# The last feed-forward of a twelve-layer decoder, taken as steps in the slots of the attention ahead of it

## The chip, the cores and the metric

The kernel runs on one core of one Trainium2 chip. The core has five engines with queues of their own: PE (TensorE, matmuls and transposes, results in PSUM), DVE (VectorE), ACT (ScalarE), POOL (GpSimd) and SP (SyncE, here a queue for DMA issues). The metric is the device time of one execution in microseconds (us): the median of the runs shown. The kernel before has 2451.33 us, the median of 3 runs from 2450.39 to 2455.79.

## The reference, cut to what matters

A residual stream x of shape (8, 256, 256) in f32 passes twelve sublayers, x = x + f(norm(x)). The last three count here:

```
x = x + L3_attn(layernorm(x))             # 16 heads of 16, causal, low-rank scores
h = rmsnorm(layernorm(x)) @ W_in.T + b_in  # L3_xattn; plus a smoothed, regathered context ctx
x = x + h + depool(rmsnorm(ctx), lens)
h = relu(layernorm(x) @ w1 + b1)           # L3_ffn: 256 -> 1024 -> 256
x = x + h @ w2 + b2
```

The output is x. Everything is f32, with 8 batches of 256 rows, 2048 rows in all.

## The kernel before, in words

**Layout.** x lies in SBUF as eight tiles x[b] of 128 partitions by 2 by 256 (the two halves of a batch's rows). xn holds the normed rows and xnT their transpose, 128 by 2 by 2048. Both are shared by all layers.

**Order.** The program is written in Python and a scheduler orders each engine's queue when it is built: of the instructions whose inputs are ready by its own model it takes the one that stands first in the program. A DMA or a POOL operation can so be issued ahead of others that the program lists earlier. While `self.pinned` is "both", which holds in `attend`, the PE and DVE instructions keep the order of the program; ACT, POOL and SP stay free. Tiles come from pools with a number of buffers for each name; a new tile waits until the last reader of the buffer that it takes over is done. A layer has a pool of its own in SBUF, left and right in turn, and PSUM pools (`banks`): in this attention 6 banks of name mm, each 128 by 512 f32.

**The attention's slots.** `attend` runs over slots n; one slot is one head of one batch, 8 x 16 = 128 of them, total = 128. In slot n PE makes the scores of head n (line 342), their maxima go through DVE (line 356), and the transposed scores of head m = n - lag, lag = 10, are made again with the maximum inside (line 373) and go through ACT's exponential (line 385). What else has to happen is put into a dictionary `todo` by slot: `prepare` (projections, 15 to 9 slots ahead of a batch), `together` every fourth slot (transposes of queries, `blend` with the values on line 396, `divide`), and what `finish`, `following` and `behind` add after a batch's last `divide`. Slots go on until todo is empty.

**The layer beside it.** `l3_xattn` has no slots of its own: its per-batch steps `beside` (load ctx, squares on ACT, scaling, smoothing, counting, places; slots 0 to 8 of a batch) and `behind` (product, add, second norm) are taken in the attention's slots. Batch b divides last in slot 16b + 31; `finish` needs 6 slots more, the norm that follows 8, then come the product 2 slots later and the second norm's parts 4, 6, 7, 10 and 12 slots later. For the last batch that is slots 143, 159 and 161 to 169. `ctx` has two buffers, and so the load of batch b + 2 waits for `scaled` of batch b.

**The last feed-forward.** `l3_ffn` is a layer of its own after the attention. It loads w1 and w2 into the ring of three weight buffers, b1 and b2 on ACT's queue, and adds b2 to every x[b] on POOL (line 1921, 8 operations). Then, for four blocks of 512 rows (two batches each): eight matmul pairs of w1 and xnT into a bank each (line 1926) with a Relu on ACT into fh (line 1927, two buffers of 16 KB a partition), and for each batch of the block two chains of eight matmuls of fh and w2 into one bank (line 1933) and one add to x on DVE (`add_to_x`, line 268). `store` then sends the eight x[b] out, 256 KB each, as each becomes ready (line 1939).

Lines 166 (`mm`), 71 (the wrapper of the pinned engines) and 268 are helpers, so many operations share them in the profile.

Of the kernel before, what the change touches and what calls it, by code (L numbers as in the profile page):

```python
# [21 lines left out]
F32 = mybir.dt.float32  # L22
# [9 lines left out]
P = 128  # L32
# [45 lines left out]
class Decoder:  # L78
# [214 lines left out]
        for i, (dst, wide, g) in enumerate(parts):  # L293
            self.nc.scalar.copy(dst, ps[:, i, :])  # L294

    def attend(self, pool, nh, dh, prepare, finish, scale=1.0, causal=False, beside=None, behind=None):

# [161 lines left out]
        while todo or now[0] <= total + lag + 1:  # L461
            n = now[0]
            m = n - lag
            if halves:
                score(n, 0), weigh(m, 0), score(n - 1, 1), weigh(m - 1, 1)
                peak(n - 1), exponentials(m - 1)
            else:
                score(n, 0), weigh(m, 0), score(n, 1), weigh(m, 1)
                peak(n), exponentials(m)
            for fn in todo.pop(n, ()):  # L470
                fn()
            now[0] += 1
        self.pinned = False

# [1238 lines left out]
    def l3_attn(self, pool):  # L1713

        nc, dram = self.nc, self.dram
        w = self.weights(dram["l3a_w"])
        wq, wo = k_of(w[:, :512], 2), k_of(w[:, 512:1024], 2)
        wqv = k_of(w[:, 1024:2048], 2)  # L1720
        wk = k_of(self.weights(dram["l3a_wk"])[:, :1024], 2)
        lsr = self.plain("l3a_lsr", pool)
        bq, bkw = self.plain("l3a_bq", pool), self.plain("l3a_bkw", pool)
        bv, bo = self.row("l3a_bv", pool), self.row("l3a_bo", pool)
        bqv = pool.tile([P, 512], F32, tag="bqv", name="bqv", bufs=1)
        nc.gpsimd.tensor_copy(bqv[:, D:], bv)
        nc.vector.tensor_tensor(
            bkw, bkw, self.cst[:, C_ONE17 : C_ONE17 + 1].to_broadcast([P, 4]), ALU.add
        )

        a = pool.tile([P, 2, P], F32, tag="a", name="a", bufs=1)
        wide_bq = pool.tile([P, 2, P], F32, tag="wide_bq", name="wide_bq", bufs=1)
        pa, pb = self.bank(2, P), self.bank(2, P)
        pw = self.bank(2, 2, P)
        for f in range(2):
            fs = slice(f * P, (f + 1) * P)
            self.mm(pa[:, f, :], (lsr[:, fs], lsr[:, D + f * P : D + (f + 1) * P]))
        heads = self.cst[:, C_HEADS : C_HEADS + P].unsqueeze(1).to_broadcast([P, 2, P])
        nc.vector.tensor_tensor(a, pa, heads, ALU.mult)
        nc.vector.tensor_copy(wide_bq, bq.unsqueeze(2).to_broadcast([P, 2, P]))  # L1740
        for f in range(2):
            for i in range(2):
                self.mm(pw[:, i, f, :], (wq[:, f, i * P : (i + 1) * P], a[:, f, :]))
            self.mm(pb[:, f, :], (wide_bq[:, f, :], a[:, f, :]))
        nc.vector.tensor_copy(wqv[:, :, :D], pw.rearrange("p i f n -> p i (f n)"))
        nc.vector.tensor_copy(bqv[:, :D], pb.rearrange("p f n -> p (f n)"))
        qs = self.wides("q", 3, 16, [16])
        vs = self.wides("v", 3, 16, [16])
        two = lambda r: r.unsqueeze(1).to_broadcast([P, 2, D])
        split = lambda r: r.rearrange("p (h d) -> p h d", d=16).unsqueeze(1).to_broadcast([P, 2, 16, 16])  # L1750

        def prepare(b):
            xT = self.xnT[:, :, b * S : (b + 1) * S]
            q, v = qs[b % 3], vs[b % 3]
            live = {}

            def project(t):
                qv = self.bank(512)
                self.mm(qv, *[(xT[:, k, t * P : (t + 1) * P], wqv[:, k, :]) for k in range(2)])
                for dst, c in ((q, 0), (v, D)):  # L1760
                    self.dve(nc.vector.tensor_tensor(
                        dst[:, t, :, :16], qv[:, c : c + D].rearrange("p (h d) -> p h d", d=16),
                        bqv[:, c : c + D].rearrange("p (h d) -> p h d", d=16), ALU.add,
                    ))

            def keys(j):
                if j == 0:
                    live["kT"] = pool.tile([P, 4, S], F32, tag="kT", name="kT", bufs=3)
                kT = live["kT"]
                pk = self.bank(2, S)  # L1770
                for i in range(2):
                    g = 2 * j + i
                    self.mm(pk[:, i, :], *[(wk[:, k, g * P : (g + 1) * P], xT[:, k, :]) for k in range(2)])
                for i in range(2):
                    g = 2 * j + i
                    nc.scalar.activation(kT[:, g, :], pk[:, i, :], AF.Identity, bias=bkw[:, g : g + 1])
                if j == 0:
                    nc.gpsimd.tensor_tensor(self.x[b], self.x[b], two(bo), ALU.add)
                return q, kT, v

            return [
                (15, lambda: project(0)), (13, lambda: project(1)), (11, lambda: keys(0)), (9, lambda: keys(1))
            ]

        def finish(b, o, later):
            oT = pool.tile([P, 2, S], F32, tag="oT", name="oT")

            def out():
                po = self.bank(2, D)
                for t in range(2):  # L1790
                    self.mm(po[:, t, :], *[(oT[:, k, t * P : (t + 1) * P], wo[:, k, :]) for k in range(2)])
                self.add_to_x(b, None, po)

            later(2, lambda: self.features(oT, o))
            later(4, out)
            return 6

        beside, behind = self.l3_xattn(pool)
        self.attend(pool, 16, 16, prepare, finish, 1.0 / math.sqrt(32.0), True, beside, behind)

    def l3_xattn(self, pool):


        nc, dram = self.nc, self.dram
# [36 lines left out]
        def beside(b):  # L1841
# [2 lines left out]
            live = {}  # L1844

            def squares():
                live["ctx"] = ctx = new("ctx", 2, 512)
                live["ss"] = ss = self.small.tile([P, 2], F32, tag="css", name="css")
                nc.sync.dma_start(ctx, dram["ctx"][b].rearrange("(h p) d -> p h d", p=P))
                for t in range(2):  # L1850
                    scalar.activation(self.junk, ctx[:, t, :], AF.Square, accum_out=ss[:, t : t + 1])
                gpsimd.tensor_scalar(ss, ss, 1.0 / 512, 1e-5, op0=ALU.mult, op1=ALU.add)
                gpsimd.tensor_tensor(ss, ss, self.minus, ALU.pow)

            def scaled():
                live["u"] = u = new("u", 2, D)
                for t in range(2):
                    vector.scalar_tensor_tensor(
                        u[:, t, :], live["ctx"][:, t, :D], live["ss"][:, t : t + 1], ginit, op0=ALU.mult, op1=ALU.mult
                    )  # L1860
# [32 lines left out]
        def behind(b, later):  # L1893
# [12 lines left out]
            later(2, product)  # L1906
            for wait, fn in zip((4, 6, 7, 10, 12), self.following(b, norm=after)):
                later(wait, fn)
            if b == B - 1:
                later(12, lambda: setattr(self, "next", after))  # L1910

        return beside, behind

    def l3_ffn(self, pool):
        nc, dram = self.nc, self.dram
        w1 = k_of(self.weights(dram["l3f_w1"]), 2)
        w2 = k_of(self.weights(dram["l3f_w2"]), 8)
        b1 = self.plain("l3f_b1", pool)
        b2 = self.row("l3f_b2", pool)
        for b in range(B):  # L1920
            nc.gpsimd.tensor_tensor(self.x[b], self.x[b], b2.unsqueeze(1).to_broadcast([P, 2, D]), ALU.add)
        for blk in range(4):
            hT = pool.tile([P, 8, 512], F32, tag="fh", name="fh")
            for i in range(8):
                ps = self.bank(512)
                self.mm(ps, *[(w1[:, k, i * P : (i + 1) * P], self.xnT[:, k, bass.ts(blk, 512)]) for k in range(2)])
                nc.scalar.activation(hT[:, i, :], ps, AF.Relu, bias=b1[:, i : i + 1])
            for j in range(2):
                po = self.bank(2, D)
                for t in range(2):  # L1930
                    c = (2 * j + t) * P
                    self.mm(
                        po[:, t, :], *[(hT[:, i, c : c + P], w2[:, i, :]) for i in range(8)],
                    )
                self.add_to_x(2 * blk + j, None, po)

    def store(self):
        for b in range(B):
            self.nc.sync.dma_start(self.out[b].rearrange("(h p) d -> p h d", p=P), self.x[b])

    def run(self):
# [11 lines left out]
        with tc.tile_pool(name="between", bufs=1, reuse_waits="tile") as self.between:  # L1955
            with tc.tile_pool(name="l1f_hbm", bufs=1, space=bass.MemoryType.DRAM) as self.hbm:
                self.layers(self.l1_ffn, self.l2_attn)
        self.layers(self.l2_xattn, self.l2_ffn, self.l3_attn, self.l3_ffn)
        self.store()

    def layers(self, *layers):
# [171 lines left out]
```

## Time and profile before

| | |
|---|---|
| median of 3 runs | 2451.33 us (2450.39 to 2455.79) |
| the profiled execution's own time | 2458.11 us |
| its span, first to last instruction | 2456.3 us |
| PE busy | 2255.6 us (92%), 11739 instructions |
| DVE / ACT / POOL busy | 1221.8 / 889.2 / 498.8 us |
| mean granted PE clock | 0.938 |
| last feed-forward's first matmul | 2339.69 us |
| its last matmuls' add on DVE | 2452.18 us |

Times inside the profile count from the span's start. A line of the timeline or of the chain has start, duration, engine, source line, operation, output <- input, the number of operations merged into it, and in brackets how long the engine was idle before it and what ended that. A line of the windows has, for each engine, busy time and number of instructions, then the granted PE clock as a share of the full one, the share of time in which the DMA engines were busy, and GB/s. "issue" is time in which nothing that the profile shows was waited for.

### The profile page before, as it was taken

The numbers are of one execution on the slowest core, as the hardware profiler recorded it, in microseconds if no ns is written. First come the engines' busy times: TensorE is split into PE (matmuls) and PEld (weight loads), VectorE is DVE, ScalarE is ACT, GpSimd is POOL, SyncE is SP. The second block draws the span as 40 slices with busy tenths as digits, with TensorE's granted clock in tenths as the row PEclk, the third lists the DMA queues.
The fourth block names the chain that finished last, engine by engine and source line by source line (L and its number), as shares of the span: only waits on it lengthen the run. The fifth ranks groups of instructions, "written<-read, shape, count | busy, mean of one in ns | idle before, by whom it ended". The sixth has DMA issues, their size and how long they took to land. (4 is left out here: it accounts for less than half of the span.)

```text
span 2456.3 us, 32071 instructions
## 1 busy us (share of the span) xinstructions
PE 2255.6 (92%) x11739; PEld 1438.1 (59%) x11739; DVE 1221.8 (50%) x3136; ACT 889.2 (36%) x2182; POOL 498.8 (20%) x712
## 2 busy tenths in 40 slices
PE   7888889999999999889899987866999989999999
PEld 4555555666655555555557864544665555566556
DVE  5666553434323235676566537984453234555400
ACT  3433422334211113466114426764552114434311
POOL 3211333221000002221125534440212100000010
PEclk9999999999999999899899996886999998899899
DMA  3000000001100000121515571100111010000000
GB/s 128 1 1 1 30 14 26 18 10 37 55 13 26 13 18 13 49 66 36 211 38 154 164 175 52 46 18 1 53 36 32 0 52 18 10 18 18 4 13 22
DMA packets 56539, 103.69 MB, mean 42 GB/s; under 512 B 7624, under 2 KB 40224, under 8 KB 54720
## 3 DMA queue, kind: packets, MB, share of 16 engines
q1 hardware_dynamic: 44688, 75.90, 9.1%
q0 software_dynamic: 7680, 20.98, 3.7%
q10 hardware_dynamic: 4016, 4.76, 0.6%
q8 instruction: 95, 1.56, 0.3%
q14 instruction: 60, 0.49, 0.1%
HBM read 84.64 MB, written 16.78 MB: 41 GB/s over the span
## 5 line engine op out<-in xcount | busy, mean ns | idle before, releaser
L166 PE MATMUL mm<-xnT,w 128*128 128x512 f32 (+1 forms) x1104 | 475.0, 576 | 1.4 <-ACT xnT L249 0.7
L342 PE MATMUL mm<-kT,qT 17*128 17x256 f32 (+2 forms) x1536 | 322.3, 413 | 15.7 <-DVE q L360 12.7
L166 PEld LDWEIGHTS mm<-xnT,w 128*128 128x128 f32 x1104 | 210.5, 193 | 200.9 <-issue 191.6
L373 PE MATMUL mm<-qT,kT 18*128 18x256 f32 (+2 forms) x1536 | 310.8, 407 | 1.4 <-ACT p L385 1.2
L385 ACT ACTIVATE p<-mm 128x512 f32<-128x512 f32 (+1 forms) x384 | 211.9, 561 | 264.0 <-PE mm L373 138.5
L360 DVE TENSOR_REDUCE q<-mm 128x2 f32<-128x512 f32 x256 | 172.3, 688 | 166.9 <-PE mm L373 148.8
L342 PEld LDWEIGHTS mm<-kT,qT 17*128 17x128 f32 (+1 forms) x1536 | 179.0, 193 | 115.0 <-issue 41.1
L557 ACT ACTIVATE hT<-mm 128x512 f32<-128x512 f32 x104 | 62.1, 597 | 431.0 <-PE mm L166 412.0
L558 DVE TENSOR_TENSOR hT<-hT,mm 128x512 f32<-128x512 f32 x104 | 71.4, 686 | 278.3 <-PE mm L166 278.2
L533 PE MATMUL acc<-w,hT 128*128 128x256 f32 x832 | 195.5, 379 | 1.0 <-DVE x L268 1.0
L533 PEld LDWEIGHTS acc<-w,hT 128*128 128x128 f32 x832 | 157.9, 190 | 62.9 <-issue 41.8
L373 PEld LDWEIGHTS mm<-qT,kT 18*128 18x128 f32 (+1 forms) x1536 | 172.8, 191 | 13.7 <-issue 5.2
L232 POOL TENSOR_SCALAR rstd<-mv 128x2 f32<-128x2 f32 x64 | 12.2, 191 | 816.9 <-DVE mv L228 466.8
L396 PE MATMUL acc<-p,v 128*32 128x256 f32 (+2 forms) x1536 | 141.1, 389 | 0.0
L268 DVE TENSOR_TENSOR x<-x,mm 128x512 f32<-128x512 f32 x40 | 27.3, 686 | 193.1 <-PE mm L166 193.0
L294 ACT COPY qT<-tp 128x256 f32<-128x256 f32 x256 | 83.7, 376 | 84.0 <-PE tp L290 83.0
L1295 POOL DMA_INDIRECT xg<-xd,token x96 | 93.1, 969 | 98.3 <-PE tp L1418 62.7
L356 DVE TENSOR_REDUCE q<-mm 128x1 f32<-128x128 f32 (+1 forms) x256 | 78.7, 352 | 56.4 <-PE mm L331 56.2
L166 PE MATMUL mm<-wall,xT 128*128 x384 | 101.1, 387 | 2.3 <-DVE xT L1420 1.2
L290 PE MATMUL tp<-ident,q 128*128 128x128 f32 x512 | 90.6, 299 | 3.3 <-ACT qT L294 1.9
L396 PEld LDWEIGHTS acc<-p,v 128*32 128x32 f32 (+1 forms) x1536 | 61.7, 122 | 47.0 <-issue 21.6
L290 PEld LDWEIGHTS tp<-ident,q 128*128 128x128 f32 x512 | 60.7, 149 | 44.6 <-issue 32.0
(428 smaller groups left out, 3842.4 us busy)
## 6 DMA issues: line engine op xcount, KB each, us to landing
wall<-in_l1f_w SPq DMA_DIRECT2D x8, 1536.0 KB
yd<-y SPq DMA_DIRECT2D x96, 128.0 KB
kT<-in_ctxK SPq DMA_DIRECT2D x16, 512.0 KB
v<-in_ctxV SPq DMA_DIRECT2D x16, 512.0 KB
w<-in_l0f_w SPq DMA_DIRECT2D x8, 768.0 KB
cT<-in_ctxT SPq DMA_DIRECT2D x8, 512.0 KB
ctx<-in_ctx SPq DMA_DIRECT2D x8, 512.0 KB
w<-in_l2f_w SPq DMA_DIRECT2D x3, 768.0 KB
```

The costliest lines, as they stand in the source:

```text
L166: self.pe(self.nc.tensor.matmul(out, lhsT=lhsT, rhs=rhs, start=i == 0, stop=i == len(pairs) - 1))
L290: self.pe(self.nc.tensor.transpose(ps[:, i, t * P : (t + 1) * P], flat[:, t, g * P : (g + 1) * P], self.ident))
L294: self.nc.scalar.copy(dst, ps[:, i, :])
L342: self.pe(nc.tensor.matmul(ps[n][:, S * t : S * t + w], lhsT=qTs[n // hp][r, t * P : (t + 1) * P], rhs=kT[r, g, :w], start=t == 0 or not c ...
L356: self.dve(nc.vector.tensor_reduce(to[:, t : t + 1], bank[:, cols], axis=AX.X, op=ALU.max, negate=True))
L360: self.dve(nc.vector.tensor_reduce(to, bank.rearrange("p (t s) -> p t s", t=2), axis=AX.X, op=ALU.max, negate=True))
L373: self.pe(nc.tensor.matmul(ps[m, 1][:, 256 * k : 256 * k + w], lhsT=kT[r, g, k * P : (k + 1) * P], rhs=qTs[m // hp][r, S - w :], start=k = ...
L385: nc.scalar.activation(p, bank[:, :n3], AF.Exp, scale=scale)
L396: self.pe(nc.tensor.matmul(acc[r, S - w :], lhsT=v[:, k, (G * hp + i) % nh, :], rhs=live_p[G * hp + i][:, 256 * k : 256 * k + w], start=k ...
L533: self.pe(nc.tensor.matmul(acc[:, t, :], lhsT=hT[:, t * P : (t + 1) * P], rhs=units[i][2], start=i == 0 and t % 2 == 0, stop=i == len(unit ...
L558: nc.vector.tensor_tensor(hT, hT, u, ALU.mult)
L1295: (engine or self.nc.gpsimd).indirect_dma_start(out=dst, out_offset=None, in_=src, in_offset=bass.IndirectOffsetOnAxis(ap=rows, axis=0))
```

## The change

`l3_ffn` becomes a function that the attention calls. It returns a generator of 48 steps and a function `biased(b)`. A step is one first product with its Relu (eight to a block) or one chain of eight matmuls of the second product (four to a block). `attend` gets the generator as `then` and takes one step at the end of each slot with m > total; the steps left over are taken in a row after the last slot. `biased(b)`, the POOL add of b2, is put 11 slots behind each batch's `last`, between its second norm's scaling (10) and its transposes (12). fh has one buffer and lies in the attention's pool, as b1 and b2 do; ctx and u get one buffer. The feed-forward's banks are the attention's six. The batch that ends last adds and stores its two halves singly.

```diff
@@ attend
+            if then and m > total:
+                next(then, None)
             now[0] += 1
@@ l3_attn
-        beside, behind = self.l3_xattn(pool)
-        self.attend(pool, 16, 16, prepare, finish, 1.0 / math.sqrt(32.0), True, beside, behind)
+        rest, biased = self.l3_ffn(pool)
+        beside, behind = self.l3_xattn(pool, biased)
+        self.attend(pool, 16, 16, prepare, finish, 1.0 / math.sqrt(32.0), True, beside, behind, rest)
+        for _ in rest:
+            pass
@@ l3_xattn
-                live["ctx"] = ctx = new("ctx", 2, 512)
+                live["ctx"] = ctx = new("ctx", 2, 512, bufs=1)
-                live["u"] = u = new("u", 2, D)
+                live["u"] = u = new("u", 2, D, bufs=1)
...
-            if b == B - 1:
-                later(12, lambda: setattr(self, "next", after))
+            later(11, lambda: biased(b))
@@ l3_ffn
-        w1 = k_of(self.weights(dram["l3f_w1"]), 2)
-        w2 = k_of(self.weights(dram["l3f_w2"]), 8)
         b1 = self.plain("l3f_b1", pool)
         b2 = self.row("l3f_b2", pool)
-        for b in range(B):
+
+        def biased(b):
             nc.gpsimd.tensor_tensor(self.x[b], self.x[b], b2.unsqueeze(1).to_broadcast([P, 2, D]), ALU.add)
...
+        def steps():
+            w1 = k_of(self.weights(dram["l3f_w1"]), 2)
+            w2 = k_of(self.weights(dram["l3f_w2"]), 8)
+            for blk in range(4):
+                hT = pool.tile([P, 8, 512], F32, tag="fh", name="fh", bufs=1)
+                for i in range(8):
+                    ps = self.bank(512)
+                    self.mm(ps, *[(w1[:, k, i * P : (i + 1) * P], self.xnT[:, k, bass.ts(blk, 512)]) for k in range(2)])
+                    nc.scalar.activation(hT[:, i, :], ps, AF.Relu, bias=b1[:, i : i + 1])
+                    yield
+                for j in range(2):
+                    po = self.bank(2, D)
+                    for t in range(2):
+                        c = (2 * j + t) * P
+                        self.mm(po[:, t, :], *[(hT[:, i, c : c + P], w2[:, i, :]) for i in range(8)])
+                        if blk == 3 and j == 1:
+                            self.add_to_x(7, t, po[:, t, :])
+                        yield
+                    if blk < 3 or j < 1:
+                        self.add_to_x(2 * blk + j, None, po)
+
+        return steps(), biased
@@ store
-        for b in range(B):
+        for b in range(B - 1):
             self.nc.sync.dma_start(self.out[b].rearrange("(h p) d -> p h d", p=P), self.x[b])
+        for h in range(2):
+            self.nc.sync.dma_start(self.out[B - 1, h * P : (h + 1) * P], self.x[B - 1][:, h, :])
@@ run
-        self.layers(self.l2_xattn, self.l2_ffn, self.l3_attn, self.l3_ffn)
+        self.layers(self.l2_xattn, self.l2_ffn, self.l3_attn)
```

## The prediction

> **What bounds the kernel now.** I read the page's busy shares first (PE 92%, all else at most 50%), then the chain of waits over the last 150 us, then the busy time by windows. The end of the chain:
>
> ```profile
> 2312.14 1.70 PE acc L396 x15
> 2313.84 1.05 PE tp L71 x4
> ...
> 2335.39 2.62 DVE xn L71 x2
> 2338.06 0.92 PE tp L71 x3
> 2339.05 0.59 ACT xnT L249
> 2339.69 112.39 PE mm L166 x384
> 2452.18 0.69 DVE x L268
> ```
>
> The last feed-forward is one unbroken PE run of 112.4 us that starts only when the last batch's second norm has been turned (the xnT copy at 2339.05). It is bounded by PE alone, so it gets no shorter; it can only start earlier. What lies ahead of it:
>
> ```profile
> 2306.00:2312.00 6.00, 6.00 (x35) 3.14 (x27) 1.45 (x5) 2.24 (x6) 0.88 (x2) 0.51 0.00 0
> 2312.00:2318.00 6.00, 6.00 (x34) 4.86 (x34) 1.64 (x6) 1.26 (x3) 0.00 (x0) 0.64 0.00 0
> 2318.00:2324.00 6.00, 3.75 (x19) 2.75 (x17) 3.26 (x9) 0.59 (x1) 0.88 (x2) 1.00 0.00 0
> 2324.00:2330.00 6.00, 4.13 (x14) 3.30 (x15) 1.70 (x6) 1.17 (x2) 0.88 (x2) 0.72 0.03 6
> 2330.00:2336.00 6.00, 2.37 (x11) 1.73 (x10) 2.40 (x6) 0.00 (x0) 1.53 (x3) 1.00 0.06 19
> 2336.00:2340.00 4.00, 1.66 (x5) 0.99 (x6) 2.00 (x2) 0.58 (x1) 4.00 (x4) 0.60 0.00 0
> 2340.00:2344.00 4.00, 4.00 (x6) 1.67 (x6) 0.00 (x0) 0.49 (x1) 4.00 (x5) 0.55 0.00 0
> 2344.00:2350.00 6.00, 6.00 (x16) 2.65 (x15) 0.00 (x0) 2.26 (x4) 1.23 (x2) 1.00 0.00 0
> ```
>
> The columns are window, length, busy time of PE, weight loads, DVE, ACT and POOL with counts, PE clock, and transfers. From 2318 to 2340 PE is busy 11.9 of 22 us, part of that at a low clock; then the feed-forward's first 4 us run at 0.55. That idle stretch is the drain of the attention: batch 7's chain of product, norm, product, norm with nothing beside it.
>
> **Where the steps land.** A step is taken when m > total, so n - 10 > 128: slots 139 to 169 (batch 7 divides in slot 143; its second norm is turned in slot 143+6+8+12 = 169). That is 31 of 48 steps. Slot 139's first work is the last blend, which ends at 2313.84, so the first step starts there.
>
> **PE from 2313.84 on.** In the view by tile each f32 matmul is two records. Block to block the feed-forward's own DVE adds stand at 2362.63 and 2390.18, 27.55 us apart, so four blocks are 110.2 us: a first-product step 1.72 us (its Relus are 1.72 apart), a second-product step 3.44 us. The attention's remaining PE work, by its full-clock pieces in the chain, is 4 turns x 0.44, features 0.44, one pair of transposes 0.22, two products x 3.65, out 1.92: 11.6 us. The clock is low until about 2316.3 (the spacing of the 128x256 records falls from 0.31 to 0.215 us there); that costs 2.5 us x 0.5 = 1.2 us. The sum is 123.0 us, and PE ends at 2436.8 instead of 2452.2: **-15.4 us**.
>
> TensorE: Matmul & The Clock Gate of the Trainium skill (section on the warmup) says the full clock returns after some 3.4 us of sustained work. Counted from 2313.84 that would be 2317.2 and 0.5 us more than the row gives; no row of before shows the gate with this mix.
>
> This needs PE never to wait in those slots. The tightest pair is features (slot 145) to out (147): two steps, 3.4 us, against the 0.59 us copy and 0.68 us PE wait seen at 2320. Out to turn (147 to 157) took 4.2 us and now has ten steps, 24 us. Blocks 0 to 2 read only batches 0 to 5, normed by slot 137; block 3 comes after slot 169, behind 5 steps (15.5 us) of block 2. ACT needs 0.69 us per step of 1.72, and no table load stands between its copy at 2339.05 and the first Relu. One buffer of fh costs nothing: a block's first Relu comes behind that block's first matmuls, which PE issues after the old block's last. DVE's eight adds run in PE's order.
>
> **The transfers.** The weights are taken from the ring in slot 139 of the program, but the queue's view shows them issued as soon as a buffer is free:
>
> ```profile
> 1983.79 0.33 SPq L125 DMA_DIRECT2D w<-in_l3f_w  x1
> 2015.56 188.24 SPq L1849 DMA_DIRECT2D ctx<-in_ctx  x6
> 2247.72 0.34 SPq L125 DMA_DIRECT2D w<-in_l3f_w  x1
> ```
>
> w1 passed six ctx loads that stood before it in the program; w2 follows the last key projection (its matmuls end at 2247.7), 64 us before slot 139. I cost both at nothing. The two bias loads (0.33 and 0.86 us of ACT's queue) move from 2327.8 to the head of the attention near 1848, where PE waits on DVE alone: nothing. If ACT were the bound there, 1.2 us.
>
> **One ctx buffer.** Load b+1 now follows `scaled` of b; before, load b+2 did, at the same moment. So seven loads instead of six stand behind a scale, each with ACT caught on its landing:
>
> ```profile
> 2169.32 0.63 ACT L1851 ACTIVATE junk<-ctx 128x512 f32<-128x512 f32 x1 [1.58 <-DMA ctx<-in_ctx]
> ...
> 2170.48 0.38 PE L166 MATMUL mm<-ends,ones 128*128 128x256 f16 x2 [0.38 <-ACT p L385]
> ```
>
> ACT's 1.58 us becomes 0.38 us of PE. One more: **+0.4** (0 to 3.7, the link of the DMA in the chain). u with one buffer is read two slots after it is written, 14 before the next: nothing.
>
> **The biases.** Eight POOL adds (1.26 us each) leave the end and follow each batch's second norm; six fall into full attention. POOL and DVE disturb each other:
>
> ```profile
> 2335.32 9.91 POOL L1921 TENSOR_TENSOR x<-x,row_l3f_b 128x512 f32<-128x512 f32 x8
> 2335.39 2.61 DVE L71 TENSOR_SCALAR xn<-x,mv,rstd 128x256 f32<-128x256 f32 x2 [1.09 <-POOL rstd L233]
> ```
>
> Alone the same two take 0.73. At 1891.87 four took 2.55 instead of 1.46 beside one such add, so one add costs DVE at most 1.1 us: 0 to 6.5 us in all. What is queued behind on DVE are the score maxima, which read PSUM; PE waited on DVE 0.5 us in all from 2020 to 2300, so DVE has room: **+0.2**. On POOL the next batch's root can wait 1.3 us, three slots (some 7 us) ahead of its reader. The 1.9 us that the adds cost the last norm go, inside the -15.4.
>
> **The tail.** Batch 7's halves are added and stored singly. Each half's output is half of one PSUM tile, so the second half's matmuls wait for DVE to read the first. The nearest row of PE behind a DVE read of 128x256 PSUM is
>
> ```profile
> 1993.41 0.42 DVE L1739 TENSOR_TENSOR a<-mm,cst 128x256 f32<-128x256 f32 x1 [2.89 <-PE mm L166]
> 1993.89 1.22 PE L166 MATMUL mm<-a,w 128*128 128x128 f32 x4 [0.52 <-DVE a L1739]
> ```
>
> that is +0.52 (0 if it is not ordered). The last add shrinks from 0.69 to 0.42 (-0.27) and the last transfer from 256 to 128 KB; 256 KB keep the engines busy for 0.7 us in the view of transfers, so -0.35. Net **-0.1** (-0.6 to +0.5).
>
> PSUM — Partial Sum Buffer of the Trainium skill (PSUM bank collisions raise a hardware error) says that two engines may not touch one bank in the same partitions at once, even at other columns; by it the 0.52 must be paid, and without it the end would be 0.5 us earlier. No row of before reads half a bank while the other half is written.
>
> **Memory.** The attention's pool gains 16 KB for fh and about 1 KB of rows and loses 6 KB (ctx, u). If a tile used early in it now shares bytes with the preceding layer, its set-up (1847 to 1862) waits until 1984, where PE idles anyway: 0 to 5 us. Nothing in the profile says so; I take 0.
>
> **Sum.** -15.4 + 0.4 + 0.2 - 0.1 = -14.9 us. The profiled execution took 2458.11 (span 2456.3), 6.8 above the median, and the sum gives 2443.2 for it. The stretch removed is a fixed order of latencies, so I take the same difference from the median: 2451.33 - 14.9 = **2436.4 us**.
>
> **Rivals.**
>
> *One ctx buffer stalls PE (slower).* If a square stands ahead of exponentials that PE needs at once, PE loses the whole landing: 7 x 3.67 = 25.7 us, net +10.8, 2462. It decides from 14.9/7 = 2.1 us per load. For it: DMA ctx has 2.4% of the chain's last 306 us. Against: five landings in the attention cost PE under 0.4 each.
>
> *w2 comes late.* The ring could give w2 the buffer of the attention's first weights, read last by out in slot 147, where the first second-product step stands. PE would wait for the load (2247.72 to about 2252, 4.2 us) and restart at the low clock (some 1.7 us, by 2340 to 2344): gain 9.0, 2442.3. Against it: in before w2 took the key weights' buffer.
>
> *The biases hold DVE.* All 6.5 us reach PE: gain 8.6, 2442.7. Against it: DVE is busy 3.3 to 7.6 of each 10 us there.
>
> *Washed out.* Low-clock windows at other places (2030 to 2040 at 0.68, 2100 to 2110 at 0.50) shift with any new stall; three more of 3.4 us at half clock, with the tile overlap of 5 us, eat 10 us: 2446 to 2451.
>
> **How the numbers follow.** 0.2% (about what a measurement of this kernel tells from no change) is 4.9 us. Chances: forecast 0.70 (own range 2431 to 2441), w2 late 0.09, biases 0.06, washed out 0.05, slower 0.10. Faster 0.70 + 0.09 + 0.06 = 0.85, same 0.05, slower 0.10. The range takes in the two partial gains and, below, a clock better than in the profile: 2430 to 2445, leaving out 0.15 and a little.
>
> **What would show it.** In the profile after: the first xnT,w matmul of the feed-forward near 2314; PE busy throughout 2318 to 2340 at clock 1.0; PE's last matmul 15 us earlier; w2 issued near 2248; seven ctx loads from 2015 on; POOL's bias adds some 38 us apart; a gap of half a microsecond before the last 16 matmul records. Wrong would be a PE wait on w2 or fh inside the slots, ACT waits on ctx above 2 us, or the attention from 2000 to 2312 longer by more than 2 us.

## The result, and the profile after

| | before | after |
|---|---|---|
| median | 2454.19 us (2449.9 to 2466.92, 22 runs) | 2443.55 us (2435.04 to 2455.36, 22 runs) |
| ratio, 95% interval | | 0.9957 [0.9945, 0.9968] |
| profiled execution, its span | 2458.11, 2456.3 us | 2436.07, 2434.3 us |
| mean granted PE clock | 0.938 | 0.941 |

The kernel is 10.6 us faster (7.9 to 13.5 by the interval). In a second comparison it had 2446.39 against 2455.62 us, ratio 0.9954 [0.994, 0.9968]. The two profiled spans differ by 22 us, twice that. Single executions of one kernel lie some 20 us apart, and the first 1850 us, ahead of the change, alone came out 7.8 us shorter in this profile, so the spans as such say little. I cut both traces at events that stand in both kernels and compare the stretches between them.

The events, each taken at its start but for the blend, are: the first add hT<-hT,mm on DVE in the feed-forward of the layer group before (about 1855 us), the issue of the attention's first weights (w<-in_l3a_w on SP), the first ctx load that waits for a scaling, the issue of w2, the end of the last blend, and the last add to x on DVE. Below, **run-in** is the first stretch, **head** the second, **last stretch** the one from the last blend to the last add.

| stretch, us | before | after | difference |
|---|---|---|---|
| run-in: first hT add to the attention's weights | 123.43 | 120.38 | -3.05 |
| head: to the first ctx load behind a scaling | 36.94 | 43.19 | +6.25 |
| to the issue of w2 | 232.16 | 232.89 | +0.73 |
| to the end of the last blend | 66.12 | 64.65 | -1.47 |
| last stretch: to the last add | 138.34 | 122.33 | -16.01 |
| tail: to the end of the span | 4.12 | 3.42 | -0.70 |
| sum | 601.11 | 586.86 | -14.25 |

The last stretch is what the change is about. The chain of waits of the kernel after, end of the span (start, duration, engine, tile or operation, line, number merged):

```profile
2308.55 3.63 PE mm L166 x8
2312.19 0.44 PE tp L71 x4
...
2323.17 0.44 PE tp L192 x4
2323.60 22.41 PE mm L166 x88
2346.01 0.44 PE tp L71 x4
...
2385.19 41.36 PE mm L166 x152
...
2426.64 0.43 DVE x L268
...
2427.12 3.74 PE mm L166 x16
...
2430.88 0.42 DVE x L268
```

Where before had the DVE norms and the short turns of the drain, PE now goes from matmul to matmul from the end of the last blend (2308.55) to 2426.55; the norms of batch 7 have left the chain. The busy time by windows of the same kernel (columns as in the prediction's table) gives PE all of its time, at the full clock:

```profile
2318.00:2340.00 22.00, 22.00 (x90) 16.39 (x89) 4.94 (x13) 3.22 (x5) 3.04 (x5) 1.00 0.04 12
```

Before, the same table had 11.9 busy us of 22. The one gap left stands ahead of the last 16 records. From the timeline of the kernel after:

```profile
2426.64 0.42 DVE L268 TENSOR_TENSOR x<-x,mm 128x256 f32<-128x256 f32 x1 [2.84 <-PE mm L166]
...
2427.12 3.72 PE L166 MATMUL mm<-w,fh 128*128 128x256 f32 x16 [0.58 <-DVE x L268]
2430.88 0.42 DVE L268 TENSOR_TENSOR x<-x,mm 128x256 f32<-128x256 f32 x1 [3.81 <-PE mm L166]
```

The queue of SP shows the transfers as forecast, seven ctx loads behind a scaling (one merged row) and w2 long before its first use:

```profile
2011.01 226.31 SPq L1855 DMA_DIRECT2D ctx<-in_ctx  x7
2243.90 0.34 SPq L125 DMA_DIRECT2D w<-in_l3f_w  x1
```

What was not forecast is the head. From the timeline of the kernel after:

```profile
1967.91 0.33 ACTq L138 DMA_DIRECT2D in_l3a_lsr<-in_l3a_lsr  x1
...
1978.29 0.44 ACTq L138 DMA_DIRECT2D in_l3x_gcol<-in_l3x_gcol  x1
1979.81 9.96 POOL L1781 TENSOR_TENSOR x<-x,row_l3a_bo 128x512 f32<-128x512 f32 x8 [1.55 <-DMA row_l3a_bo<-in_l3a_bo]
1985.75 1.62 DVE L1817 TENSOR_SCALAR win<-win,in_l3x_gcol 128x256 f32<-128x256 f32 x2 [6.68 <-DMA in_l3x_gcol<-in_l3x_gcol]
1989.03 1.23 PE L166 MATMUL mm<-a,w 128*128 128x128 f32 x4 [5.54 <-DVE a L1742]
```

The loads of the attention's rows (lsr and the others), which stood at 1847 to 1859 before, beside the earlier layer, are issued only at 1967.91. DVE then stands 6.68 us for gcol, and PE waits 5.54 us for the product `a` that is queued behind it on DVE (0.52 us before).

### The profile page after: what moved, and what is told of

It reads as the page before. It is cut to its first block, busy times and chain, and to the rows that moved or that the text cites. A ratio compares the mean times of both kernels' runs of the same rounds, so it can differ in the third digit from the quotient of the medians.

```text
span 2434.3 us, 32056 instructions
## 1 busy us (share of the span) xinstructions
PE 2241.4 (92%) x11739; PEld 1432.1 (59%) x11739; DVE 1217.8 (50%) x3137; ACT 888.0 (36%) x2182; POOL 500.1 (21%) x712
## 5 line engine op out<-in xcount | busy, mean ns | idle before, releaser
L374 PEld LDWEIGHTS mm<-qT,kT 18*128 18x128 f32 (+1 forms) x1536 | 172.9, 191 | 13.5 <-issue 4.9
L268 DVE TENSOR_TENSOR x<-x,mm 128x512 f32<-128x512 f32 (+1 forms) x41 | 27.5, 672 | 175.9 <-PE mm L166 175.9
```

Of the source, the lines that this page charges most:

```text
L374: self.pe(nc.tensor.matmul(ps[m, 1][:, 256 * k : 256 * k + w], lhsT=kT[r, g, k * P : (k + 1) * P], rhs=qTs[m // hp][r, S - w :], start=k = ...
```

## The experiments

All compare traces by the stretches above; times are medians with the ratio to the kernel before, run beside them. Where only one execution is given, the reading rests on its trace. In the compiled kernels the attention's pool ends at byte 217696 of a partition before and at 228992 after, and the earlier layer's hT tiles lie at 225248 to 229344: fh now covers 3744 of their bytes.

**fit: the pool kept clear of hT.** Names that are not alive together share buffers, so the pool ends at byte 224896, 352 short of hT. Nothing else of the changed kernel is touched.

```diff
-        a = pool.tile([P, 2, P], F32, tag="a", name="a", bufs=1)
-        wide_bq = pool.tile([P, 2, P], F32, tag="wide_bq", name="wide_bq", bufs=1)
+        a = pool.tile([P, 2, P], F32, tag="dep", name="a", bufs=3)
+        wide_bq = pool.tile([P, 2, P], F32, tag="dep", name="wide_bq", bufs=3)
...
-        li, lf, end = one_of("li", [B, S], I32), one_of("lf", [B, S]), one_of("end", [B, S])
+        li, lf = pool.tile([B, S], I32, tag="plug", name="li"), pool.tile([B, S], F32, tag="plug", name="lf")
+        end = one_of("end", [B, S])
```

> Computes the same; two small set-up pairs (a and wide_bq, li and lf) share buffers with tiles used later, so the attention's pool is 4 KB smaller and ends 352 bytes short of the preceding feed-forward's hT. Theory (the pool overlaps hT by 3.7 KB, and so all of its set-up is issued only when that layer's last hT is taken): the set-up is issued as in the kernel before, behind the layer's head; from the load of the attention's first weights to the first ctx load behind a scale takes 37 us as before instead of 43, the rest as in the changed kernel; 6 us less than the changed kernel, ratio to before 0.993. Rival (the two bias loads that were put ahead in ACT's queue delay the set-up): they stand there still, so no change, 43 us and a ratio of 0.9957.

Measured: 2444.64 us (2437.27 to 2455.14), ratio 0.9944 [0.9923, 0.9965]. Head 37.05 us, as before the change, and in the timeline of fit the loads stand beside the earlier layer again, the bias b2 among them:

```profile
1841.35 0.32 ACTq L138 DMA_DIRECT2D in_l3a_lsr<-in_l3a_lsr  x1
...
1851.21 0.34 ACTq L132 DMA_DIRECT2D row_l3f_b<-in_l3f_b  x1
```

Shared bytes are what moved the set-up. fh alone lies on hT, but the whole set-up came late. The run-in is 123.42 us, also as before the change: the 3.05 us that the kernel after had gained there are gone with the cause of the 6.25. The next run says why. The 6 us and the ratio of 0.993 that were expected did not come; the interval holds the 0.9957 of the kernel after as well, so the times alone do not show that fit is faster than it.

**pad_before: the kernel before, with a tile of 8 KB more, 640 bytes of it on hT.** No load is moved in the program, no step and no other buffer; the tile is not used further.

```diff
         self.attend(pool, 16, 16, prepare, finish, 1.0 / math.sqrt(32.0), True, beside, behind)
+        pad = pool.tile([P, 8, 256], F32, tag="pad", name="pad", bufs=1)
+        nc.gpsimd.memset(pad[:, 0, :1], 0.0)
```

> The kernel before with one thing more: an 8 KB tile in the attention's pool, of which one column is cleared at the end, so that the pool reaches 640 bytes into hT. Theory (overlap alone delays the set-up): 6 us slower than before, ratio 1.0025, the stretch from the first weights' load to the first ctx load behind a scale 43 us instead of 37, the end untouched. Rival (bias loads in ACT's queue): they are where they were, so 1.000 and 37 us.

Measured: 2458.65 us against 2459.85, ratio 1.0001 [0.9984, 1.0019]. The head grew to 40.51 us, so shared bytes alone delay the set-up and cost 3.6 us there, not the 6 that were expected; and the run-in shrank to 120.38, so that the sum of the two is 160.89 us against 160.37 and the time did not move. The delayed set-up takes POOL's adds of the row bo out of the earlier layer. In that layer each of its three turns from one block to the next has four DVE scalings, and before, one of the adds fell on them. The timeline of before, at the first turn:

```profile
1891.87 2.55 DVE L238 TENSOR_SCALAR xn<-x,mv,rstd 128x256 f32<-128x256 f32 x4 [1.22 <-POOL rstd L233]
1892.69 1.26 POOL L1778 TENSOR_TENSOR x<-x,row_l3a_bo 128x512 f32<-128x512 f32 x1
1894.16 0.87 PE L248 MATMUL tp<-ident,xn 128*128 128x128 f32 x4 [0.89 <-DVE xn L238]
```

and of after, at the same turn, where all eight adds stand at 1979.81:

```profile
1884.13 1.54 DVE L238 TENSOR_SCALAR xn<-x,mv,rstd 128x256 f32<-128x256 f32 x4 [1.22 <-POOL rstd L233]
1884.92 1.36 PE L248 MATMUL tp<-ident,xn 128*128 128x128 f32 x8
```

The scalings take 1.54 us instead of 2.55, and PE's wait of 0.89 us is gone; three such turns are the 3.05 us. SBUF — State Buffer of the Trainium skill (SBUF: two separate sides) calls the port pair that VectorE and GpSimd share an exclusive lock: of a GpSimd operation and a VectorE operation of the kinds that use the pair, the one that starts first has it for its whole instruction and the other stands. The 1.01 us lost here, beside an add of 1.26, fit that; which of the two started first the rows don't show.

**loads_behind: the changed kernel with the two bias loads behind the cross-attention's set-up**, to see whether they account for the other 2.7 us of the head (43.19 against 40.51).

```diff
-        rest, biased = self.l3_ffn(pool)
-        beside, behind = self.l3_xattn(pool, biased)
+        beside, behind = self.l3_xattn(pool, lambda b: biased(b))
+        rest, biased = self.l3_ffn(pool)
```

> The changed kernel with the set-up of the cross-attention written before that of the feed-forward, so that the two bias loads stand behind the loads of gcol, brow, ginit and the lengths on ACT's queue; the bytes shared with the earlier layer stay. Head is the time from the issue of the attention's first weights to the first ctx load behind a scale: 36.94 us before, 43.19 after, 40.5 with shared bytes alone. Theory (the two loads ahead of gcol cost the other 2.7 us): head 40.0 to 41.0, and DVE's wait for gcol gone or below 4 us. Rival (the rest comes from more bytes being shared, whatever the order of the loads): head 42.5 or more.

Measured: one execution of 2433.96 us, head 44.25 us, so the theory's 40.0 to 41.0 fell. The gcol load went out at 1974.30 and DVE waits 0.71 us for it, yet the head is longer. The timeline of loads_behind, DVE's queue:

```profile
1980.44 2.54 DVE L1817 TENSOR_SCALAR win<-win,in_l3x_gcol 128x256 f32<-128x256 f32 x2 [0.71 <-DMA in_l3x_gcol<-in_l3x_gcol]
1986.43 0.29 DVE L1823 TENSOR_SCALAR row_l3x_ginit<-row_l3x_ginit 128x256 f32<-128x256 f32 x1 [3.45 <-DMA row_l3x_ginit<-in_l3x_ginit]
1986.64 1.35 DVE L1834 CAST lf<-li 8x256 f32<-8x256 int32 x1
1988.02 1.63 DVE L1835 TENSOR_TENSOR_SCAN end<-one,lf 8x256 f32<-8x256 f32 x1
1989.69 1.17 DVE L1836 TENSOR_SCALAR lf<-end 8x256 f32<-8x256 f32 x1
1990.79 0.41 DVE L1742 TENSOR_TENSOR a<-mm,cst 128x256 f32<-128x256 f32 x1
```

The wait has moved to the next load of the set-up (3.45 us for ginit), and three more set-up operations now precede `a` on DVE. So the order of the bias loads isn't the cause by itself: with the set-up late, whichever of its loads lands last holds DVE, and `a` with it. What exactly makes the head 43.2 with the bias loads and 40.5 in pad_before no run shows. The rows have one candidate, the load of w1 (1 MB). In loads_behind it goes out ahead of ginit's load:

```profile
1977.97 0.33 SPq L125 DMA_DIRECT2D w<-in_l3f_w  x1
1979.06 0.39 ACTq L132 DMA_DIRECT2D row_l3x_ginit<-in_l3x_ginit  x1
```

In pad_before it goes out behind it:

```profile
1985.29 0.39 ACTq L132 DMA_DIRECT2D row_l3x_ginit<-in_l3x_ginit  x1
1986.69 0.34 SPq L125 DMA_DIRECT2D w<-in_l3f_w  x1
1990.39 0.29 DVE L1819 TENSOR_SCALAR row_l3x_ginit<-row_l3x_ginit 128x256 f32<-128x256 f32 x1 [0.97 <-DMA row_l3x_ginit<-in_l3x_ginit]
```

From ginit's issue to DVE's use of it are 7.37 us with w1 ahead and 5.10 without. In the kernel after it is gcol's load that stands behind w1 (1977.30 and 1978.29), and 7.46 us pass until DVE goes on.

**no_steps: the changed kernel with no step in a slot**; all 48 follow in a row.

```diff
-            if then and m > total:
+            if then and m > 2 * total:
```

> The changed kernel with all 48 steps behind the last slot instead of 31 in the slots; everything else of the change stays. Theory (the gain is PE's idle drain filled by steps): PE is idle again for some 10 of the last 25 us of the attention, PE's last stretch is 12 to 15 us longer than in the changed kernel (a few matmuls can still slip ahead of the last transposes, and the last norm is freed of the bias adds), and with the 6 us lost at the attention's head it is no faster than before: ratio 1.000 to 1.003. Rival (the gain comes from the moved biases and the single stores, the steps add little): ratio 0.996 to 0.998.

Measured: 2455.88 us (2444.09 to 2465.1, 12 runs), ratio 0.9981 [0.9962, 0.9999], between the theory's and the rival's. The last stretch is 132.40 us: the steps in the slots are worth 10.1 of the 16.0 us, less than the 12 to 15 expected, and the drain is back (windows of no_steps: PE, weight loads, DVE, ACT, POOL, clock, transfers):

```profile
2332.00:2338.00 6.00, 2.13 (x9) 1.66 (x10) 2.83 (x9) 0.77 (x2) 2.16 (x3) 0.76 0.01 3
2338.00:2344.00 6.00, 6.00 (x18) 4.60 (x17) 0.61 (x1) 0.41 (x1) 0.00 (x0) 0.67 0.00 0
```

The other 5.9 us come without any step. Part of it is seen in the timeline of no_steps: since the feed-forward is no longer a layer that begins after the attention, its first matmuls are issued while DVE still does the last norm.

```profile
2343.18 2.74 PE L166 MATMUL mm<-xnT,w 128*128 128x512 f32 x6
2346.93 0.30 PE L71 MATMUL tp<-ident,xn 128*128 128x128 f32 x1 [1.00 <-DVE xn L71]
```

**bias_only: the kernel before with the b2 adds taken after each batch's norm**, as in the change, and nothing else of it.

```diff
+            later(11, lambda: self.nc.gpsimd.tensor_tensor(self.x[b], self.x[b], b2.unsqueeze(1).to_broadcast([P, 2, D]), ALU.add))
...
-        for b in range(B):
-            nc.gpsimd.tensor_tensor(self.x[b], self.x[b], b2.unsqueeze(1).to_broadcast([P, 2, D]), ALU.add)
```

> The kernel before with the eight bias adds alone moved behind each batch's second norm; the feed-forward stays a layer of its own behind the attention. The stretch from the last blend's end to the last DVE add is 138.3 us before and 132.4 in the run without steps in the slots. Theory (the adds cost the last norm 1.9 us, and the rest of those 5.9 us is matmuls that slip ahead of the last transposes once the layer shares the attention's banks): 136.4 us. Rival (all of the 5.9 us come from the moved adds): 132.4.

Measured: one execution of 2454.45 us; last stretch 136.22, 2.1 us less than before. In its last norm the scaling of the two halves is back to the short time (timeline of bias_only):

```profile
2334.21 0.74 DVE L71 TENSOR_SCALAR xn<-x,mv,rstd 128x256 f32<-128x256 f32 x2 [1.09 <-POOL rstd L233]
```

So of the 5.9 us some 2.1 are the biases and 2.7 the early matmuls. The remaining 1.1 us no run takes apart; the rows point at the clock. The feed-forward's first 24 matmul records take 12.49 us in the kernel before (from 2339.69, at 0.55 to 2344) and the 24 from 2348.25 on take 10.46 in no_steps, where the clock is 1.00; against these 2.0 us, the last product ahead of them takes 1.0 us longer in no_steps.

**fit_banks: fit, with a PSUM bank of its own for the last half.**

```diff
+                        if blk == 3 and j == 1 and t:
+                            po = self.bank(2, D)
                         self.mm(po[:, t, :], *[(hT[:, i, c : c + P], w2[:, i, :]) for i in range(8)])
```

> As fit, and the last batch's two halves have a PSUM bank each. Theory (the second half's matmuls wait for DVE to read the first half because both lie in one bank's tile): the gap of 0.58 us before the last 16 matmul records is gone, 0.6 us less than fit in the profile's tail (last product's first matmul to the span's end), not resolved in the times, ratio 0.993. Rival (PE waits there for something else, fh or w2): the gap stays.

Measured: 2442.06 us (2440.57 to 2448.02), ratio 0.9932 [0.991, 0.9954]. In its timeline DVE's idle time between the two last adds is 2.96 us instead of 3.81, and PE's 0.58 us gap is gone:

```profile
2437.03 0.42 DVE L268 TENSOR_TENSOR x<-x,mm 128x256 f32<-128x256 f32 x1 [2.96 <-PE mm L166]
```

The gap came from the two halves' shared tile, which is one bank; whether the tile or the bank is what orders them, this run doesn't tell, since it parts both. PSUM — Partial Sum Buffer of the Trainium skill (PSUM bank collisions raise a hardware error) asks that engines be kept apart by bank and not by address. Keeping to that order cost 0.58 us here.

**bias_end: fit_banks, with the eight b2 adds after the attention** instead of behind each norm.

```diff
+        for b in range(B):
+            biased(b)
         for _ in rest:
             pass
...
-            later(11, lambda: biased(b))
```

> As fit_banks, with all eight bias adds behind the last slot instead of spread over the attention. From the first ctx load behind a scale to the load of w2 takes 232.2 and 231.3 us in the two kernels that add the biases at the end, and 232.6 to 233.3 in the four that spread them. Theory (the adds disturb DVE inside the attention): 231.7, some 1 us less than fit_banks, with the rest as there. Rival (the extra ctx load or the clock makes that difference): 232.6 to 233.3 still.

Measured: 2445.08 us in one execution. From the first ctx load behind a scaling to w2 232.64 us, to the last blend 64.64, last stretch 121.46; fit_banks has 232.61, 64.63 and 121.47. The adds in the slots cost nothing that these two traces show.

**ctx2: fit_banks with a second ctx buffer**, its space won by sharing three more names.

```diff
-                live["ctx"] = ctx = new("ctx", 2, 512, bufs=1)
+                live["ctx"] = ctx = new("ctx", 2, 512)
```

> As fit_banks, with two ctx buffers again; three more set-up tiles share buffers so that the pool keeps its size. Theory (one buffer adds a seventh load behind a scale, at 0.4 us of PE): six loads behind a scale instead of seven, PE's waits on the exponentials one fewer and 0.4 us less, the same stretch to w2 within 0.5 us. Rival (one buffer makes every square late): ACT's waits on ctx fall by more than 3 us and the stretch by more than 1.

Measured: 2439.09 us in one execution. ACT waits 9.5 us for six landings instead of 10.8 for seven (in the kernels before and after: 9.1 for six, 10.6 for seven), but PE waits hardly less. PE's waits for the exponentials, kernel ctx2 from 2018 to 2310 (us in total, times, longest):

```profile
PE mm L166 <- ACT p L386: 1.6, 5, 0.4
PE mm L374 <- ACT p L386: 1.2, 7, 0.2
```

the kernel after, with seven, from 2011 to 2300:

```profile
PE mm L166 <- ACT p L386: 1.5, 5, 0.3
PE mm L374 <- ACT p L386: 1.2, 7, 0.2
```

and fit_banks, with seven, from 1990 to 2450:

```profile
PE mm L166 <- ACT p L386: 1.7, 6, 0.5
PE mm L374 <- ACT p L386: 1.2, 7, 0.2
```

One wait fewer than fit_banks, as the theory had it, but 0.1 us and not 0.4.

The stretch to w2 is 1.2 us shorter in ctx2, outside the theory's 0.5, and the one to the last blend 1.6 us. The number of buffers doesn't sort the kernels, though: with two, the stretch to w2 is 232.16 us in the kernel before, 232.74 in bias_only, 231.33 in pad_before and 231.38 in ctx2; with one, 232.61 in fit_banks and 230.63 in loads_behind. The clock goes with it here: over the 240 us behind that ctx load its mean is 0.943 in ctx2 and pad_before against 0.935 in fit_banks, and in the 30 us from 270 us on, 1.00 in both against 0.94. So I put the 1.2 us down to the clock and not to the buffer.

**early: fit_banks with steps ten slots sooner.**

```diff
-            if then and m > total:
+            if then and n >= total:
```

> As fit_banks, with steps from slot 128 on, where the scores end, instead of 139: 42 of 48 in the slots. Theory (PE has no idle time left there, at most a low clock while the slots hold 18-row matmuls alone): from w2's load to the last DVE add 184 to 186 us instead of 186.1, ratio 0.991 to 0.993. Rival (more steps beside the second scores hold up the exponentials and the banks): 188 us or more and a ratio above 0.994.

Measured: 2437.2 us (2434.54 to 2451.69), ratio 0.9921 [0.9896, 0.9946]. Issue of w2 to the last add 185.36 us against 186.10 in fit_banks.

**The three beside each other**: after, fit_banks and early, with the same executions of the kernel before for all.

> The changed kernel, the same work, run beside the two tuned versions so that the three share their runs of the kernel before. Theory (the head of the last attention pays 6.2 us for the shared bytes, the end pays 0.5 us for the shared bank, and what the parts gain is 16.0 us): 10 to 11 us below before, ratio near 0.9957. Rival (the 0.9957 was a chance of the clock's windows): a ratio above 0.998 or below 0.993.

> The pool kept clear of the earlier layer and the last block's halves in two banks. Theory: 6.7 us below the changed kernel of the same call, ratio near 0.9930. Rival (the head's 6.2 us come back elsewhere, since PE then enters the attention with a colder clock): within 2 us of the changed kernel.

> The same, with the steps allowed ten slots sooner. From the traces of the first runs, issue of w2 to the last DVE add takes 185.4 us with the early steps and 186.1 without: theory (PE is full either way, so earlier steps only swap places): within 1.5 us of the kernel without early steps in this call. Rival (early steps remove a low-clock window near the start of the feed-forward): 3 to 6 us below it, ratio near 0.991.

| | median | ratio | first hT add to the end of the span |
|---|---|---|---|
| after_again | 2446.39 us (2440.14 to 2452.3, 11 runs) | 0.9954 [0.994, 0.9968] | 593.21 us |
| fit_banks_again | 2443.21 us (2433.78 to 2448.15, 8 runs) | 0.9942 [0.9923, 0.9962] | 589.04 us |
| early_again | 2441.87 us (2433.5 to 2445.47, 6 runs) | 0.9945 [0.9924, 0.9965] | 582.20 us |

The expectation of 6.7 us for fit_banks fell: it is 3.2 us at the medians and 4.2 in the traces. I had counted from the issue of the attention's weights and so missed the run-in; with it, 6.25 - 3.05 + 0.58 = 3.8 us, which lies between the two. Early and fit_banks are 1.3 us apart at the medians, within the 1.5 of the theory. All three beat the kernel before; the intervals don't separate them from each other.

## Why the prediction came out as it did

It gave 2436.4 us, a gain of 14.9, and the median is 2443.55, a gain of 10.6. Of the 7.2 us between, 2.9 are the kernel before itself, which had 2454.19 in this comparison and not 2451.33; 4.3 are a gain that is smaller. By its own steps:

- **Where the steps land, and PE from the last blend on: -15.4.** Right in size. The last stretch gave -16.0 with the 0.58 us of the shared bank in it, so -16.6. The excess is as large as the 1.2 us that I charged for a low clock up to 2316; in the kernel after the windows have 1.00 from 2300 on. But I put the whole gain on the steps, with 1.9 for the biases in it; no_steps shows 10.1 for the steps in the slots, and 5.9 for what comes free without them, 2.1 of it the biases.
- **The transfers: nothing.** Right for w2: issued at 2243.90, no PE wait for it, and the rival of a late w2 falls. What w1 costs in the head, where it now meets the late set-up loads, is open (loads_behind). The bias loads cost PE nothing in fit, where they stand where I had put them; PE's waits in the run-in are those of before. What they cost in the head of the kernel after, where the set-up is late, is not shown.
- **One ctx buffer: +0.4.** Seven landings as forecast, none above 1.8 us on ACT, and PE's waits for ACT unchanged (1.5 and 1.2 us in both kernels): 0, the lower bound. The rival in which PE loses a whole landing falls.
- **The biases: +0.2.** 0 by bias_end (one execution each), and the rival in which they hold DVE falls. POOL's adds came some 38 us apart in full attention, as said.
- **The tail: -0.1.** 0.58 us of wait for 0.52, and the end 0.70 shorter for 0.62.
- **Memory: 0, bounded by 5.** This is the term that was mis-sized. The sentence on it named the mechanism (a tile that shares bytes with the layer ahead, the set-up held until 1984) and the place, and took zero because nothing in the profile spoke for it; a profile shows no addresses. It is 6.25 us at the head, above the bound. The sentence also took for granted that PE idles there anyway, but PE's product `a` hangs on DVE behind the set-up's loads. And it didn't see the other side, 3.05 us won in the layer ahead, where POOL's adds no longer fall on DVE's scalings. Net +3.2 us. The sign that was to show a slower attention began at 2000, behind this place, and could not have caught it.

The measured terms sum to -16.0 - 0.7 + 3.2 = -13.5 us; the two middle stretches, +0.73 and -1.47, have no cause of the change's that a run shows. The times say -10.6, from -13.5 to -7.9. A second profile of the same work, after_again, has the terms again: run-in 120.38 us, head 43.38, last stretch 123.01. But from w2 to the last blend it takes 69.87 us instead of 64.65, at a clock of 0.67 to 0.75 from 2300 to 2330, and its sum of 593.21 us is only 7.9 below the kernel before, where the first profile is 14.3 below. The difference between the terms and the times is smaller than this one of the clock between two executions, so the account is not settled to better than some 3 us; the rival of gains washed out by the clock holds to that extent and no further. There is luck in the time, too: the 3.05 us won in the run-in, which the prediction didn't see, made up half of the 6.25 that it took at nothing. Without them the median would stand near 2446.6 us, above the range of 2430 to 2445.

## What to carry to other kernels

A loop whose drain leaves an engine idle is the place for the next layer's steps, and the gain can be read ahead by adding up the work that the engine has left: 15.4 us here, and 16.0 measured. But a tile placed in a longer-lived pool has an address as well as a size: one that overlaps a live tile of the layer ahead can hold the set-up of its whole pool, which the profile of before cannot show, so work the layout out and price the late set-up by what stands behind its loads on each engine. Compare stretches between events that both kernels have, and begin them early enough: a delay at one place moved work out of another, and a cut 120 us too late made 3.2 us look like 6.2.

## What was unexpected of the hardware

**The clock falls while PE is busy, at places that change from one execution to the next.** The same kernel, fit_banks, profiled twice. The first execution, windows:

```profile
2300.00:2310.00 10.00, 10.00 (x62) 5.72 (x61) 2.67 (x9) 3.98 (x9) 0.89 (x2) 0.83 0.01 2
2310.00:2320.00 10.00, 10.00 (x69) 5.26 (x69) 2.80 (x10) 4.72 (x11) 2.16 (x3) 1.00 0.00 1
```

The second one:

```profile
2300.00:2310.00 10.00, 10.00 (x59) 5.49 (x62) 3.17 (x11) 2.53 (x6) 0.89 (x2) 0.67 0.00 1
2310.00:2320.00 10.00, 10.00 (x52) 5.32 (x45) 1.95 (x7) 2.81 (x6) 2.15 (x3) 0.57 0.00 0
```

PE counts as busy for all 10 us of each, at 1.00 or at 0.57. The stretch from w2 to the last blend took 64.63 us in the one and 69.94 in the other. TensorE: Matmul & The Clock Gate of the Trainium skill (Part 1: The HAM clock gate) says that the monitoring window runs free and that the clock drops after an idle window. The first agrees with a place that moves; an idle window no row here shows, though the ends of matmuls are modelled in this profile, so that a busy time may hide gaps. Whether the early steps of `early` keep this stretch at the full clock is open: both of its profiles have 185.36 us from w2 to the last add, where fit_banks has 186.10 and 192.02.

**Small DVE operations stretch beside POOL.** In loads_behind the cast, the scan and the scaling of 8x256 took 1.35, 1.63 and 1.17 us beside POOL's row of adds; in fit, where no add runs then, 0.27, 0.68 and 0.28.
